# Layer 0's attention of images 0 to 6: from eight stretches of eight score tiles to five groups of thirteen

## The chip, the cores and the metric

The kernel runs on one core of one Trainium2 chip. The metric is the time of one execution on the device in microseconds (us). Three runs of the kernel before took 2767.86, 2767.95 and 2768.16 us, with a median of 2767.95. Engines are named as in the profile: PE is TensorE, PEld its weight loads, DVE is VectorE, ACT is ScalarE, POOL is GpSimd, SP is SyncE with its DMA queue.

## The reference

Eight images of 512 channels and 1024 tokens (32 by 32) in float32 pass through two attention blocks. What matters of block 0, with nh = 8 heads of ch = 64 channels:

```python
h = group_norm(x, gn_weight, gn_bias)
qkv = jnp.einsum('oc,bct->bot', w_qkv, h.reshape(B, C, T)) + b_qkv[None, :, None]
q, k, v = (qkv[:, :ch], qkv[:, ch:2 * ch], qkv[:, 2 * ch:])       # per head
weight = jnp.einsum('bct,bcs->bts', q * scale, k * scale)
weight = jax.nn.softmax(weight, axis=-1)
a = jnp.einsum('bts,bcs->bct', weight, v)
out = jnp.einsum('oc,bct->bot', w_proj, a) + b_proj[None, :, None]
return x + out
```

Block 1 is the same form with one head over all 512 channels and a group norm of 8 groups. The change touches block 0's attention and, because small products of block 1's group norm are computed in the middle of it, the place of those.

## The kernel before

The dense products (queries, keys, values, projections, and everything of block 1) are made with a Strassen-Winograd scheme, and the stages of neighbouring images are interleaved: while image b's block 0 attention runs, the block 1 norm of image b - 1 is worked in beside it. The program is written in one order. The recording layer keeps it on each engine (`keep_in_program_order` pins what could be moved), and each engine executes its own instructions in that order, waiting on semaphores for the others.

Block 0's attention of one image is `attention0` (L677). The eight heads are four pairs `hp`, the 1024 queries two halves `tb`, so there are eight stretches `(hp, tb)`, and each has eight tiles `s` of 128 keys. For one tile PE makes the scores of both heads side by side: the contraction has 64 rows, so the two heads sit in the two row halves of the array (shape 64*128 in the profile). The tile is 128 by 1024 and fills two banks of PSUM. ACT turns it into `e` with one exponential of 1024 columns (L696), DVE adds it to the running `total` of the stretch (L698 the first time, L700 after). After the eight score tiles of a stretch PE multiplies the eight `e` tiles with the values; here each head has 64 output channels, so the two heads sit in the two column halves of the array (shape 128*64), accumulating in `av`. ACT copies `av` to `a` (L719).

After every second stretch the totals of one head pair are ready. `reciprocals` (L631) sums each over the 128 partitions with a product with ones in quarters of the array (shape 128*32, tile `sums`), DVE copies the result to SBUF (`line`, L655), a DMA writes it to memory, another reads it back spread over the partitions (`cols`), DVE takes reciprocals (`recs`, L662), and two more DMAs bring them back as rows (`r`). DVE then multiplies `a` with `r` (L734), and SP stores `a` as `kept`. The last pair's scaling is moved behind the attention and done on POOL.

PSUM has eight banks. In this stage three pools of one two-bank tile hold the scores, taken in turn, and two banks (`acc_tile`) hold `av`, `sums`, and the group norm's `gmean` and `gvar`. So the scores of a tile can start when ACT has read the tile three before.

`big_tile` gives SBUF tiles of 4 KB per partition from one pool of `NBIG` = 34: images, queries, keys, values, `e` tiles, totals and factor sums all come from it.

Other work is hooked in through `extra`, sixteen lists of small steps taken in turn: an even slot between the scores and the values of a stretch, an odd slot behind its values. For images 1 to 6 the previous image's `projection2` fills them: POOL's residual additions (L1091) in slot 0, the norm's statistics on DVE in slots 1 and 3 and the store of the image to DRAM in 3, the group mean (`gmean`, L108 to 119) in slot 4, the affine factors (`gvar`, L121 to 130) in 5, and the norm's application on ACT in slots 7 and 9. The main loop adds to slots 9, 11, 13 and 15 the sums of the next products: DVE's `t_h` and `x` differences of 128 by 512 (L1028) and `inner_h` differences of 128 by 256 (L434).

Image 7, the last, goes through the same function without a store.

Of the kernel before, what the change touches and what calls it, by code (L numbers as in the profile page):

```python
# [9 lines left out]
F32 = mybir.dt.float32  # L10
I32 = mybir.dt.int32
AF = mybir.ActivationFunctionType
# [3 lines left out]
P = 128  # L16
EPS = 1e-5
ORDER = (1, 5, 2, 6, 7, 3, 4)
NBIG = 34

# [7 lines left out]
def two_attention_blocks_kernel(  # L30
# [28 lines left out]
    def matmul(*args, **kw):  # L59
        tc.keep_in_program_order(nc.tensor.matmul(*args, **kw))  # L60
# [113 lines left out]
    def main_path(ctx):  # L174
# [15 lines left out]
        def pair_tile(name):  # L190
            return big_tile(name, (P, 2, HT))

        def acc_tile(name):
            return ps_acc.tile([P, HT], F32, tag="acc", name=name)
# [433 lines left out]
            return out  # L628


        def reciprocals(totals, uid, across, direct=None):  # L631

            n = len(totals)
            sums = acc_tile(f"sums_{uid}")[:, : n * 2 * P].rearrange("p (t a b) -> p t a b", t=n, a=2)
            for t in range(n):  # L640
                for i in range(4):
                    matmul(
                        sums[ts(i, 32), t, :, :], ones, totals[t][:, :, ts(i, P)],
                        start=t == 0, stop=t == n - 1, skip_group_check=True,
                    )
            rows = all_rows[len(taken) : len(taken) + n]
            taken.extend(totals)
            line = rpool.tile([P, 2, 2, P], F32, tag="line", bufs=1, name=f"line_{uid}")[:, :n]
            queue = direct or nc.sync
            lines = lambda d: d.rearrange("t j i n -> i (t j) n"), line[0:P:32].rearrange("p t a b -> p (t a) b")  # L650
            if direct:
                nc.vector.reciprocal(line, sums)
                queue.dma_start(lines[0](rows), lines[1])
            else:
                nc.vector.tensor_copy(line, sums)  # L655
                raw_rows = rowpool.tile([n, 2, 4, P], F32, tag=f"rows{n}", name=f"rows_{uid}")
                queue.dma_start(lines[0](raw_rows), lines[1])
                cols = small.tile([P, 16], F32, tag="cols", name=f"cols_{uid}")[:, : n * 8]
                flat = lambda t: t.rearrange("t j i n -> (t j i n)").rearrange("(p m) -> p m", p=P)
                queue.dma_start(cols, flat(raw_rows))  # L660
                recs = small.tile([P, 16], F32, tag="recs", name=f"recs_{uid}")[:, : n * 8]
                nc.vector.reciprocal(recs, cols)  # L662
                queue.dma_start(flat(rows), recs)
            if across:
                r = pair_tile(f"r_{uid}")
                for j in range(2):
                    row = rows[0, j : j + 1].rearrange("j i n -> j (i n)")
                    queue.dma_start(r[:, j, :], row.to_broadcast([P, HT]))
            else:
                r = rpool.tile([P, 2, HT], F32, tag="r", bufs=1, name=f"r_{uid}")[:, :n]  # L670
                for j in range(2):
                    row = rows[:, j : j + 1].rearrange("t o i n -> o t (i n)")
                    queue.dma_start(r[ts(j, 64)], row.to_broadcast([64, n, HT]))
            return r


        def attention0(b, q, k, v, a, extra, store=None):  # L677
            n = 0
            scaled, totals, behind = [], [], []

            for hp in range(KC):
                for tb in (0, 1) if hp < KC - 1 or store else (1, 0):
                    uid = f"0_{b}_{hp}_{tb}"
                    total = pair_tile(f"sum_{uid}")
                    es = []
                    for s in range(NS):

                        sc = ps_pools[(0, 2, 1)[n % 3]].tile([P, 2, HT], F32, tag="sc", name=f"sc_{uid}_{s}")
                        n += 1
                        for j in range(2):  # L690
                            matmul(
                                sc[:, j, :], k[hp][ts(j, 64), ts(s, P)], q[hp][ts(j, 64), ts(tb, HT)],
                                start=True, stop=True,
                            )
                        e = pair_tile(f"e_{uid}_{s}")
                        nc.scalar.activation(e, sc, AF.Exp, scale=(C // 8) ** -0.5)  # L696
                        if s == 1:
                            nc.vector.tensor_add(total, es[0], e)  # L698
                        elif s > 1:
                            nc.vector.tensor_add(total, total, e)  # L700
                        es.append(e)
                    for f in extra.pop(0) if extra else ():
                        f()
                    av = acc_tile(f"av_{uid}")
                    for s in range(NS):
                        for j in range(2):
                            matmul(
                                av[ts(j, 64), :], v(s, 2 * hp + j),
                                es[s][:, j, :], start=(s == 0), stop=(s == NS - 1),
                            )  # L710
                    after = extra.pop(0) if extra else []
                    if not (store and hp == KC - 1):
                        after, scaled = [*scaled, *after], []
                    elif tb == 1:
                        after, scaled = [*after, *scaled], []
                    for f in after:
                        f()
                    dst = a[hp][:, ts(tb, HT)]
                    nc.scalar.copy(dst, av)  # L719

                    totals.append(total)
                    if hp < KC - 1 or store:
                        if tb == 0:
                            continue
                        dst = a[hp].rearrange("p (t n) -> p t n", t=2)
                    else:
                        dst = dst.rearrange("p (t n) -> p t n", t=1)
                    direct = store is None and (hp, tb) == (KC - 1, 0)
                    engine = nc.gpsimd if hp == KC - 1 and not direct else nc.vector
                    scaled = []  # L730

                    def scale(hp=hp, dst=dst, totals=totals, uid=uid, direct=direct, engine=engine, scaled=scaled):
                        r = reciprocals(totals, uid, False, nc.scalar if direct else None)
                        scaled.append(lambda: tc.keep_in_program_order(engine.tensor_tensor(dst, dst, r, ALU.mult)))  # L734
                        if store:
                            scaled.append(lambda: store(hp))

                    totals = []
                    if store and hp == KC - 1:
                        behind.append(scale)  # L740
                    else:
                        scale()

            assert not extra
            return scaled, behind


# [336 lines left out]
        def projection2(b, inner, hooks):  # L1084
# [8 lines left out]
            def store():  # L1093
# [3 lines left out]

            stats = [lambda c=c: norm.stats(c, xt[c]) for c in range(KC)]
            applies = [lambda c=c: norm.apply(nc.scalar, xt[c], xt[c], c) for c in range(KC)]
            _, _, (mean,), (affine,) = norm_hooks(norm, f"1_{b}")  # L1100
            return xt, {
                0: [lambda c=c: residual(c) for c in range(KC)], 1: stats[:2], 3: [*stats[2:], store], 4: [mean],
                5: [affine], 7: applies[:2], 9: applies[2:],
            }

        def norm_hooks(norm, uid):

# [64 lines left out]
            )  # L1172
            values1(b, zf, ef, state["r"], xt, f"1_{b}", ahead)

        x1, plan = None, {}
        for b in range(B):
            extra = [[] for _ in range(2 * 2 * KC)]
            for i, fs in later.items():
# [3 lines left out]
            if b > 0:  # L1182
                h, uid = x1, f"h1_{b - 1}"
            else:
                h, loads, applies = begun(load_x, norm0, 1, "h0")
                uid = "h0_1"
                for f in loads:
                    f()
                plan = {2 * c + 3: [f] for c, f in enumerate(applies)}
            for i, fs in plan.items():  # L1190
                extra[i] += fs
            a = channel_tiles(f"a0_{b}")
# [13 lines left out]
            psum_pools(f"attention_{b}", 1)  # L1206

            if last:
                scaled, _ = attention0(b, q, k, v, a, extra)
                for f in steps[4:7]:  # L1210
                    f()
                psum_pools(f"products_{b}", 2)
# [9 lines left out]
                break  # L1222

            kept = apool.tile([KC, P, T], F32, tag="kept", name=f"kept_{b}")
            scaled, behind = attention0(b, q, k, v, a, extra, lambda hp: nc.sync.dma_start(kept[hp], a[hp]))
            for f in ih[4:]:
                f()
            psum_pools(f"products_{b}", 2)
# [32 lines left out]
            q, k = keys_and_queries(  # L1261
                b + 1, inner, norm0, [lambda c=c: load_a(c) for c in range(KC)], [factors_of_a], q_hooks
            )
            x1, plan = projection2(b, inner_a, p_hooks)
        hf, steps = image_factors(h, f"h1_{B - 1}")
        inner, sums2 = inner_factors(hf, f"h1_{B - 1}")
        for f in steps + sums2:
# [204 lines left out]
```

## Time and profile before

The profile is one execution of 2768.3 us, 0.35 us over the median of the three runs. Its span, from the first to the last instruction, is 2765.8 us, so 2.5 us lie around it.

| engine | busy us | share of the span | instructions |
|---|---|---|---|
| PE | 2753.6 | 100% | 13436 |
| PEld | 1762.1 | 64% | 13436 |
| DVE | 2045.6 | 74% | 3214 |
| POOL | 1291.4 | 47% | 1384 |
| ACT | 998.4 | 36% | 1307 |

The granted TensorE clock is 0.999 of full speed over the span. Of PE's time, `sc` (block 0's scores) takes 456.8 us and `av` (its values) 453.4 us, each in 2048 instructions: a product in float32 is two passes of the array, each with its own weight load. Busy PE does not mean PE at its peak: matmuls overlap, and their ends are modelled. The time of a stage is read from the chain, which lists the pieces of work one behind the other, with the start of each.

### The profile page before, as it was taken

To read this page: it belongs to the slowest core of one execution; us is meant where nothing else is said; L and a number is where in the kernel's file an instruction comes from. 1 tells how busy PE (TensorE), PEld (TensorE's weight loads), DVE (VectorE), ACT (ScalarE), POOL (GpSimd) and SP (SyncE) were. 2 spreads that over 40 slices of the span, in tenths; PEclk is the share of its full clock that TensorE was granted. 3 is DMA by queue.
4 is the path that set the end of the run, shared out by engine and by line. 5 is a ranking of instruction groups with operands and counts; after the bars stand their busy time and mean duration, and the time that the engine had idled before them with its cause. 6 is when DMAs were issued, how large, how long until landed. Compare 5 with 4: busy or idle time off the path is not lost.

```text
span 2765.8 us, 36809 instructions
## 1 busy us (share of the span) xinstructions
PE 2753.6 (100%) x13436; PEld 1762.1 (64%) x13436; DVE 2045.6 (74%) x3214; ACT 998.4 (36%) x1307; POOL 1291.4 (47%) x1384
## 2 busy tenths in 40 slices
PE   9999999999999999999999999999999999999999
PEld 5437736776376853868538694486844968348585
DVE  6587777777777777777777867777678776787776
ACT  1253454214632146312453125531255313633130
POOL 2313605745067440774307752176621766146763
PEclk9999999999999999999999999999999999999999
DMA  7827412344113441144401443114521145112302
GB/s 265 253 91 252 181 32 70 138 159 166 40 63 138 170 162 32 63 161 167 150 24 63 177 182 119 32 55 184 196 98 49 58 153 216 59 54 97 142 24 74
DMA packets 126070, 332.60 MB, mean 120 GB/s; under 512 B 19831, under 2 KB 64695, under 8 KB 114362
## 3 DMA queue, kind: packets, MB, share of 16 engines
q1 hardware_dynamic: 125294, 329.75, 33.6%
q8 instruction: 108, 1.77, 0.3%
q14 instruction: 80, 0.66, 0.1%
q10 hardware_dynamic: 588, 0.42, 0.1%
HBM read 258.14 MB, written 71.99 MB: 119 GB/s over the span
## 4 chain that ended last, share of the span: by engine, by line
PE 99%; DVE 1%; DMA 0%; issue 0%; SPq 0%; DVEq 0%
PE sc L60 16%; PE av L60 16%; PE psb_av L60 6%; PE psb L60 5%; PE psa_av L60 4%; PE psc_av L60 4%; PE psc L60 4%; PE psa L60 3%; PE psb_v L60 3%; PE psb_k L60 3%; PE psb_p L60 3%; PE psb_q L60 3%; PE psb_g L60 3%; PE psb_z L60 3%; PE psc_z L60 2%; PE psa_k L60 2%
## 5 line engine op out<-in xcount | busy, mean ns | idle before, releaser
L700 DVE TENSOR_TENSOR sum<-sum,e 128x1024 f32<-128x1024 f32 x384 | 473.9, 1234 | 35.5 <-ACT e L696 0.9
L696 ACT ACTIVATE e<-sc 128x1024 f32<-128x1024 f32 x512 | 476.1, 1053 | 63.1 <-PE sc L60 62.6
L60 PE MATMUL sc<-q,k 64*128 64x512 f32 x2048 | 456.8, 596 | 0.0
L60 PE MATMUL av<-e,v 128*64 128x512 f32 x2048 | 453.4, 595 | 0.0
L60 PEld LDWEIGHTS sc<-q,k 64*128 64x128 f32 x2048 | 190.1, 185 | 245.9 <-ACT e L696 120.9
L60 PEld LDWEIGHTS av<-e,v 128*64 128x64 f32 x2048 | 141.4, 137 | 299.0 <-issue 288.2
L434 POOL TENSOR_TENSOR inner_h<-x 128x256 f32<-128x256 f32 x16 | 14.8, 924 | 415.9 <-DVE x L1028 415.9
L698 DVE TENSOR_TENSOR sum<-e,e 128x1024 f32<-128x1024 f32 x64 | 79.9, 1249 | 103.6 <-ACT e L696 103.6
L719 ACT COPY a<-av 128x512 f32<-128x512 f32 x64 | 37.5, 586 | 320.1 <-PE av L60 280.6
L126 POOL TENSOR_TENSOR rstd<-ve,mhalf 128x4 f32<-128x4 f32 x16 | 18.8, 1177 | 274.0 <-DVE ve L124 274.0
L60 PE MATMUL psb<-inner,inner_h 128*128 128x256 f32 x448 | 115.6, 380 | 0.0
L60 PE MATMUL psa_av<-e,z 128*128 128x512 f32 x256 | 112.5, 592 | 0.0
L482 ACT COPY psb_v<-psa_v 128x512 f32<-128x512 f32 (+1 forms) x28 | 14.5, 517 | 232.5 <-DVE x L845 176.6
L60 PEld LDWEIGHTS psb<-inner,inner_h 128*128 128x128 f32 x448 | 84.5, 190 | 13.6 <-POOL inner L449 2.1
L60 PE MATMUL psb_z<-w_z,inner_h 128*128 128x128 f32 x672 | 87.5, 276 | 0.0
L60 PE MATMUL psb_g<-inner_h,w_m 128*128 128x256 f32 x336 | 84.9, 381 | 0.0
L776 ACT ACTIVATE e<-e 128x1024 f32<-128x1024 f32 x64 | 65.1, 1052 | 46.7 <-DVE e L766 25.6
L60 PEld LDWEIGHTS psb_z<-w_z,inner_h 128*128 128x128 f32 x672 | 81.4, 192 | 0.5
L60 PEld LDWEIGHTS psa_av<-e,z 128*128 128x128 f32 x256 | 47.4, 190 | 53.6 <-issue 51.7
L771 POOL TENSOR_TENSOR e<-e,e 128x512 f32<-128x512 f32 x64 | 79.3, 1271 | 2.0 <-DVE e L766 1.8
L571 POOL TENSOR_TENSOR v<-v,v 128x256 f32<-128x256 f32 x28 | 20.1, 726 | 125.3 <-DVE u_v L566 121.3
L820 POOL TENSOR_TENSOR t<-e,t 128x1024 f32<-128x1024 f32 x32 | 78.4, 2482 | 0.0
(443 smaller groups left out, 6138.0 us busy)
## 6 DMA issues: line engine op xcount, KB each, us to landing
r<-all_rows SPq DMA_DIRECT2D x78, 256.0 KB
x<-in_x SPq DMA_DIRECT2D x36, 512.0 KB
h<-in_x SPq DMA_DIRECT2D x32, 512.0 KB
spill<-x SPq DMA_DIRECT2D x32, 512.0 KB
x<-spill SPq DMA_DIRECT2D x32, 512.0 KB
out<-x SPq DMA_DIRECT2D x63, 256.0 KB
kept<-a SPq DMA_DIRECT2D x28, 512.0 KB
again<-kept SPq DMA_DIRECT2D x28, 512.0 KB
```

The source lines that it names most:

```text
L60: tc.keep_in_program_order(nc.tensor.matmul(*args, **kw))
L126: nc.gpsimd.tensor_tensor(rstd, ve, mhalf, ALU.pow)
L434: pin(engine.tensor_tensor(dst, x, y, ALU.subtract))
L482: nc.scalar.copy(ps["b"], ps["a"])
L571: nc.gpsimd.tensor_tensor(d, x, y, ALU.add)
L696: nc.scalar.activation(e, sc, AF.Exp, scale=(C // 8) ** -0.5)
L698: nc.vector.tensor_add(total, es[0], e)
L700: nc.vector.tensor_add(total, total, e)
L719: nc.scalar.copy(dst, av)
L771: nc.gpsimd.tensor_tensor(blocks(dst, r, cc)[0], blocks(x, r, cc)[0], blocks(y, r, cc)[0], ALU.add)
L776: nc.scalar.activation(e[c, cc, r], e[c, cc, r], AF.Exp, scale=scale)
L820: on = lambda *a: lambda: tc.keep_in_program_order(nc.gpsimd.tensor_tensor(*a))
```

## The change

`attention0` is rewritten around a flat list of 64 tiles, (stretch, s) in the old order. For images 0 to 6 it is cut into groups of `GROUP` = 13: tiles 0 to 12, 13 to 25, 26 to 38, 39 to 51 and 52 to 63. A group first makes all its scores, then all its values, across the borders of the stretches. Image 7 keeps groups of 8. The slots are still taken in turn, one when a stretch's last score tile is made and one when its last value product is made; in groups of 13 the order of these events is scores of stretch 0, values of 0, scores of 1 and 2, values of 1 and 2, scores of 3, values of 3, scores of 4 and 5, values of 4 and 5, scores of 6 and 7, values of 6 and 7.

The products of `sums` (head pairs 0 to 2) and of the norm (`gmean` behind group 0, `gvar` behind group 1) move to the ends of groups, and write a tile of the score pools, taken in turn with the score tiles, instead of an `acc_tile`. The sums of head pairs 0, 1 and 2 stand behind groups 1, 2 and 3. For image 7 `gmean` and `gvar` stand behind its second and third stretch. The statistics all move to slot 0, the store to slot 1, the second half of the norm's application to slot 10 (9 for image 7). For image 0 the applications move from slots 3, 5, 7, 9 to 4, 5, 7, 10. `NBIG` rises by one to 35.

```diff
-NBIG = 34
+GROUP = 13
+NBIG = 35
...
-        def reciprocals(totals, uid, across, direct=None):
+        def reciprocals(totals, uid, across, direct=None, tile=None):
...
-            sums = acc_tile(f"sums_{uid}")[:, : n * 2 * P].rearrange("p (t a b) -> p t a b", t=n, a=2)
+            sums = acc_tile(f"sums_{uid}") if tile is None else tile[:, 0, :]
+            sums = sums[:, : n * 2 * P].rearrange("p (t a b) -> p t a b", t=n, a=2)
...
+            size = GROUP if store else NS
...
+            def place():
+                n = places[0] % 3
+                places[0] += 1
+                return ps_pools[(0, 2, 1)[n]].tile([P, 2, HT], F32, tag="sc", name=f"sc_0_{b}_{places[0]}")
...
+            def scores(i, s):
...
+                sc = place()
+                for j in range(2):
+                    matmul(
+                        sc[:, j, :], k[hp][ts(j, 64), ts(s, P)], q[hp][ts(j, 64), ts(tb, HT)],
+                        start=True, stop=True,
+                    )
+                e = es[i, s] = pair_tile(f"e_{uid}_{s}")
+                nc.scalar.activation(e, sc, AF.Exp, scale=(C // 8) ** -0.5)
+                if s == 1:
+                    nc.vector.tensor_add(total, es[i, 0], e)
+                elif s > 1:
+                    nc.vector.tensor_add(total, total, e)
+                if s == NS - 1:
+                    slot()
...
+            for start in range(0, len(tiles), size):
+                group = tiles[start : start + size]
+                for i, s in group:
+                    scores(i, s)
+                for i, s in group:
+                    values(i, s)
+                for f in edges.pop(0) if edges else ():
+                    f(place)
+                while waiting:
+                    waiting.pop(0)(due, place())
...
-            _, _, (mean,), (affine,) = norm_hooks(norm, f"1_{b}")
+            steps = [
+                [lambda place: norm.group_mean(place()[:, 0, :KC])], [lambda place: norm.affine(place()[:, 0, :KC])],
+            ]
             return xt, {
-                0: [lambda c=c: residual(c) for c in range(KC)], 1: stats[:2], 3: [*stats[2:], store], 4: [mean],
-                5: [affine], 7: applies[:2], 9: applies[2:],
-            }
+                0: [*(lambda c=c: residual(c) for c in range(KC)), *stats], 1: [store], 7: applies[:2], 9 if b + 2 == B else 10: applies[2:],
+            }, steps
...
-                plan = {2 * c + 3: [f] for c, f in enumerate(applies)}
+                plan = {i: [f] for i, f in zip((4, 5, 7, 10), applies)}
```

More of the change, by code (lines that the diff above doesn't have):

```diff
@@ L674, in reciprocals @@
             return r
[L677 to L744, printed above, removed]
@@ new lines, in attention0, with slot, values, done @@
+        def attention0(b, q, k, v, a, extra, store=None, edges=()):
+            places, scaled, behind, waiting, due = [0], [], [], [], []
+            edges = list(edges)
+            size = GROUP if store else NS
+            order = [
+                (hp, tb) for hp in range(KC) for tb in ((0, 1) if hp < KC - 1 or store else (1, 0))
+            ]
+            tiles = [(i, s) for i in range(len(order)) for s in range(NS)]
+            es, av, totals = {}, {}, {}
+            def place():
+                n = places[0] % 3
+                places[0] += 1
+                return ps_pools[(0, 2, 1)[n]].tile([P, 2, HT], F32, tag="sc", name=f"sc_0_{b}_{places[0]}")
+            def slot():
+                for f in extra.pop(0) if extra else ():
+                    f()
+            def scores(i, s):
+                hp, tb = order[i]
+                uid = f"0_{b}_{hp}_{tb}"
+                if s == 0:
+                    totals[i] = pair_tile(f"sum_{uid}")
+                total = totals[i]
+                sc = place()
[12 more added lines that the diff above has]
+                    slot()
+            def values(i, s):
+                hp, tb = order[i]
+                if s == 0:
+                    av[i] = acc_tile(f"av_0_{b}_{hp}_{tb}")
+                for j in range(2):
+                    matmul(
+                        av[i][ts(j, 64), :], v(s, 2 * hp + j), es[i, s][:, j, :], start=(s == 0), stop=(s == NS - 1),
+                    )
+                if s == NS - 1:
+                    done(i)
+            def done(i):
+                hp, tb = order[i]
+                uid = f"0_{b}_{hp}_{tb}"
+                last = hp == KC - 1
+                if not (store and last):
+                    while due:
+                        due.pop(0)()
+                slot()
+                if store and last and tb == 1:
+                    while due:
+                        due.pop(0)()
+                dst = a[hp][:, ts(tb, HT)]
+                nc.scalar.copy(dst, av[i])
+                if not last or store:
+                    if tb == 0:
+                        return
+                    dst = a[hp].rearrange("p (t n) -> p t n", t=2)
+                    which = [totals[i - 1], totals[i]]
+                else:
+                    dst = dst.rearrange("p (t n) -> p t n", t=1)
+                    which = [totals[i]]
+                direct = store is None and (hp, tb) == (KC - 1, 0)
+                engine = nc.gpsimd if last and not direct else nc.vector
+                def scale(into, tile=None):
+                    r = reciprocals(which, uid, False, nc.scalar if direct else None, tile)
+                    into.append(lambda: tc.keep_in_program_order(engine.tensor_tensor(dst, dst, r, ALU.mult)))
+                    if store:
+                        into.append(lambda: store(hp))
+                if store and last:
+                    behind.append(lambda: scale(scaled))
+                elif store:
+                    waiting.append(scale)
+                elif direct:
+                    scale(scaled)
+                else:
+                    scale(due)
+            for start in range(0, len(tiles), size):
[8 more added lines that the diff above has]
+                    waiting.pop(0)(due, place())
+            assert not extra and not due
@@ L1099, in projection2 @@
             applies = [lambda c=c: norm.apply(nc.scalar, xt[c], xt[c], c) for c in range(KC)]
-            _, _, (mean,), (affine,) = norm_hooks(norm, f"1_{b}")
+            steps = [
+                [lambda place: norm.group_mean(place()[:, 0, :KC])], [lambda place: norm.affine(place()[:, 0, :KC])],
+            ]
             return xt, {
-                0: [lambda c=c: residual(c) for c in range(KC)], 1: stats[:2], 3: [*stats[2:], store], 4: [mean],
-                5: [affine], 7: applies[:2], 9: applies[2:],
-            }
+                0: [*(lambda c=c: residual(c) for c in range(KC)), *stats], 1: [store], 7: applies[:2], 9 if b + 2 == B else 10: applies[2:],
+            }, steps
         def norm_hooks(norm, uid):
@@ L1173, in layer1_rest @@
             values1(b, zf, ef, state["r"], xt, f"1_{b}", ahead)
-        x1, plan = None, {}
+        x1, plan, edges = None, {}, []
         for b in range(B):
@@ L1208, in main_path @@
             if last:
-                scaled, _ = attention0(b, q, k, v, a, extra)
+                scaled, _ = attention0(b, q, k, v, a, extra, None, [[], *edges])
                 for f in steps[4:7]:
@@ L1224, in main_path @@
             kept = apool.tile([KC, P, T], F32, tag="kept", name=f"kept_{b}")
-            scaled, behind = attention0(b, q, k, v, a, extra, lambda hp: nc.sync.dma_start(kept[hp], a[hp]))
+            scaled, behind = attention0(b, q, k, v, a, extra, lambda hp: nc.sync.dma_start(kept[hp], a[hp]), edges)
             for f in ih[4:]:
@@ L1263, in main_path @@
             )
-            x1, plan = projection2(b, inner_a, p_hooks)
+            x1, plan, edges = projection2(b, inner_a, p_hooks)
         hf, steps = image_factors(h, f"h1_{B - 1}")
```

## The prediction

> **What bounds the kernel now.** I read the page first (busy times and the chain that ended last), then that chain in order of time over one image's attention, then the weight loads of one stretch, then DVE around one border. The page gives PE 99% of the chain. DVE's running sums are long, but nothing idles long before them.
>
> ```profile
> PE 99%; DVE 1%; DMA 0%; issue 0%; SPq 0%; DVEq 0%
> L700 DVE TENSOR_TENSOR sum<-sum,e 128x1024 f32<-128x1024 f32 x384 | 473.9, 1234 | 35.5 <-ACT e L696 0.9
> ```
>
> The chain shows what a stretch costs. The first row below is a product of block 1 on the whole array: 16 passes of 512 columns in 6.87 us, 0.429 each. A score or value tile is four passes on half an array, two at a time, so 2 x 0.429 = 0.859 and eight tiles are 6.87 too.
>
> ```profile
> 1199.47 6.87 PE psa_av L60 x16
> ...
> 997.39 7.07 PE sc L60 x32
> 1004.46 7.02 PE av L60 x32
> 1011.48 7.07 PE sc L60 x32
> 1018.54 7.02 PE av L60 x32
> 1025.56 1.00 PE sums L60 x16
> 1026.56 7.07 PE sc L60 x32
> 1033.63 0.21 PE gmean L60 x4
> 1033.85 6.92 PE av L60 x32
> 1040.76 0.07 PE gvar L60 x3
> 1040.83 7.07 PE sc L60 x32
> ```
>
> So each entry into scores costs 0.20 us and each entry into values 0.15, the price of changing the array's shape: 0.35 a stretch. `gmean` between scores and values costs 0.21 - 0.10 = 0.11 (the values behind it are 0.10 shorter); `gvar` behind values, in the same shape, 0.07.
>
> The weight loads of one stretch, which starts at 1085.02 in this view, show how near ACT is to being the bound:
>
> ```profile
> L60 PE MATMUL sc<-q,k x2048: 589/589/693, 117.8 to 2456.7; 64*128 64x512 f32 x187
> ```
>
> ```profile
> 1088.18 0.19 PEld L60 LDWEIGHTS sc<-q,k 64*128 64x128 f32 x2 [0.29 <-ACT e L696]
> ...
> 1089.10 0.51 PEld L60 LDWEIGHTS sc<-q,k 64*128 64x128 f32 x4 [0.35 <-ACT e L696]
> 1090.01 0.45 PEld L60 LDWEIGHTS sc<-q,k 64*128 64x128 f32 x4 [0.41 <-ACT e L696]
> 1090.93 0.39 PEld L60 LDWEIGHTS sc<-q,k 64*128 64x128 f32 x4 [0.47 <-ACT e L696]
> ```
>
> These are the loads of tiles 4 to 7, each released by the exponential that frees its place. They are (1090.93 - 1088.18) / 3 = 0.917 us apart: ACT's pace, against PE's 0.859. Tile 7's first matmul is due at 1085.02 + 0.10 + 7 x 0.859 = 1091.13, so its load is only 0.20 ahead, and each further tile loses 0.058. A load needs 0.10: the first matmuls of a stretch, whose load nothing covers, last 693 ns and not 589. The stretch of eight ends just before ACT's pace is felt.
>
> DVE around the border behind the third head pair:
>
> ```profile
> 1068.11 1.22 DVE L734 TENSOR_TENSOR a<-a,r 128x1024 f32<-128x1024 f32 x1
> 1069.25 1.29 DVE L1028 TENSOR_TENSOR t_h<-x 128x512 f32<-128x512 f32 x2
> 1070.45 0.42 DVE L434 TENSOR_TENSOR inner_h<-x 128x256 f32<-128x256 f32 x1
> ...
> 1073.08 1.23 DVE L698 TENSOR_TENSOR sum<-e,e 128x1024 f32<-128x1024 f32 x1 [1.08 <-ACT e L696]
> 1074.41 7.87 DVE L700 TENSOR_TENSOR sum<-sum,e 128x1024 f32<-128x1024 f32 x6
> 1082.20 1.29 DVE L1028 TENSOR_TENSOR t_h<-x,t_h 128x512 f32<-128x512 f32 x2
> ...
> 1086.34 0.69 DVE L655 COPY line<-sums 128x512 f32<-128x512 f32 x1
> 1088.16 1.23 DVE L698 TENSOR_TENSOR sum<-e,e 128x1024 f32<-128x1024 f32 x1 [1.14 <-ACT e L696]
> 1090.42 0.25 DVE L662 RECIPROCAL recs<-cols 128x16 f32<-128x16 f32 x1 [1.03 <-DMA cols<-rows]
> ```
>
> `line` is already 1.3 us late here (sums end at 1085.0), which costs nothing while `sums` has a bank of its own. `recs` waits for its DMA, 4.08 us from the start of `line`, and holds DVE.
>
> **The change part by part.** Per image, times from a group's first score.
>
> *Fewer changes of shape.* Five pairs instead of eight. A pair without sums takes 14.09 (997.39 to 1011.48), 0.35 over 13.74; three go: -1.06. `gmean` stands in its own shape now, 0.07 instead of 0.21 - 0.10: -0.04 at least, -0.11 if it hides as `gvar` nearly does; I take -0.08 for images 1 to 6. The three sums stay at 1.0 each.
>
> *ACT's pace in long groups.* Tile 12's load comes 5 x 0.058 - (0.20 - 0.10) = 0.19 too late; PE waits that much in each of groups 0 to 3: +0.77. Group 4 has 12 tiles, 0.13, mostly swallowed by the stall below, during which ACT catches up: +0.03. Bounds per long group: 0.09 if a load needed no lead, 0.28 if it needs its recorded 187 ns. I take 0.10, which the trace shows for this shape. The Trainium skill, "TensorE: Matmul & The Clock Gate", section "LDWEIGHTS (loading the stationary operand)", puts a load at columns / 1.2 GHz, here 107 ns; an estimate from that page gives 0.20 a group against 0.28 by the recorded duration.
>
> A rule against the change is in the Trainium skill, "TensorEngine Tiling (Array Packing)", section "PSUM Bottleneck": packing speeds up PE but not the emptying of PSUM, which may become the bound. Read strictly, all 13 tiles would go at ACT's 0.917, 0.75 us over PE a group, 3.7 an image; but then a stretch of eight would already be 0.46 longer, and 7.07 is explained by the entry alone. The three places absorb the first eight tiles.
>
> *The small products in score places.* The third score tile of a group takes the place of the last small product, so it waits until DVE has read it, in DVE's order. The third tile's load is due 1.72 after the group's start. Behind group 0, DVE is at `gmean` after four sums of stretch 1: the seventh of stretch 0 starts 18.2 after the image's start (the statistics in front of it stand as before), five steps of 1.33 less the shorter join make 24.6; the group ends at 26 x 0.859 + 0.35 + 0.19 + 0.07 = 22.9, due 24.7. It just fits: +0.05, bounds 0 and 0.4. Behind groups 1 and 2 DVE has two to four us in hand.
>
> *The border behind group 3 is the tight one.* DVE's queue there, in the changed program's order: `line` of pair 1 at 0.1; one sum at 2.2; `recs`, held by its DMA until 0.1 + 4.1 = 4.2; seven sums from 4.4, 9.12 long (1073.08 to 1082.20): 13.5; `t_h` 1.20: 14.7; `inner_h` x4 1.47: 16.2; three sums 3.8: 20.0; `a` times `r` 1.14: 21.1; `t_h` 1.21: 22.3; eight `inner_h` 2.93 (1083.41 to 1086.34): 25.3; then `line`, read out at 25.95. The group with its sums takes 22.33 + 0.35 + 0.19 + 1.0 = 23.87, so the load is due at 25.6: PE waits 0.4. Bounds: 0 (DVE 0.4 faster) and 1.3 (`recs` 5.0 behind `line`, as behind image 0's first and last pair). I take 0.4, by the 4.0 to 4.3 of the waits on `cols` before a last pair. Behind this wait on PE stand ten score tiles and group 4's values; DVE's own sums wait with them.
>
> *At nothing.* ACT's norm applications (slots 7, 10; 4, 5, 7, 10 in image 0) and `av` copies stand behind a group's exponentials, under 11 us of values; before an exponential each application would cost about 1.05. SP's order is unchanged; the stores of `a` wait longer for DVE, and the one `e` tile that reuses a stored `a` needs it 10 us into group 4, some 8 us after it can land. `e` tiles reuse tiles whose sums are over in the group before. DVE ends group 4 no later than the sums of pair 3 need, as 11 sums fit into 21 us.
>
> **Sum.** Images 1 to 6: -1.06 - 0.08 + 0.80 + 0.05 + 0.4 = +0.11 each, +0.7. Image 0, without the norm: +0.14. Image 7: up to +0.1 for the norm's tiles. Together +0.9 on the profiled 2768.3, or 2768.9 against the median of 2767.95 (0.35 lower than the profiled run).
>
> **Rivals.** (A) *Waits vanish*: the lead is shorter and DVE in time. Per image -1.14 + 0.38 + 0.05 = -0.7, seven images -5: 2763; with no cost at all -8: 2760. For it: the smallest bounds; against it: 693 ns. (B) *DVE's queue at the fourth border* is later by 1 us (a slower DMA, or steps as long as beside POOL's work: two `t_h` took 2.35 at 1112.63 and 1.29 above): +1 x 7 on the sum, 2776. It crosses the 0.2% from 0.7 us of extra lateness on. For it: every item in that queue adds directly, and the last pair's `recs` come 4.8 after `line`; against it: POOL is nearly idle there. (C) *ACT's pace from the first tile*: 64 x 0.058 = 3.7 an image instead of 0.8: +20, 2788. Against it: 7.07. (D) *Waits of the longer-living tiles* (DMA, SBUF tiles) that I count as covered: like B in size.
>
> **How the numbers follow.** 0.2% is 5.5 us, about what a measurement of this kernel tells from no change. Likeliest, gains and waits nearly cancel: 0.72, 2768.9, own range 2764 to 2773. A beyond 5.5 us: 0.07. B and D: 0.18. C: 0.03. The range 2763 to 2777 leaves out part of A, and of B and D what is over 2777, and C. Faster 0.07, same 0.72, slower 0.21.
>
> **What would show it.** In the changed profile: pieces of 13 score tiles of 11.55 us (11.17 + 0.20 + 0.19) and of 13 value tiles of 11.3; in images 0 to 6 a wait of PE for DVE's `line` L657, seven times, about 0.4; nothing new outside the attention. The prediction is wrong if score pieces are near 11.9 (ACT binds earlier), or if that wait is over 1 us or absent.

## The result, and the profile after

The changed kernel takes 2776.37 us (median of eight runs, 2773.68 to 2778.99); beside it the kernel before took 2767.94. The ratio is 1.003, 95% interval 1.0019 to 1.0041: slower, by 8.4 us or 0.3%, where the prediction called 0.2% a difference (the interval's lower end, 0.19%, just touches that). Its runs lie 5.3 us apart, where those of the kernel before lay 0.7 us apart. The profiled execution took 2774.31 us with a span of 2772.5, 6.0 and 6.7 us more than the profiled one of before.

The chain of work that ended last, summed by engine, from the page of the changed kernel:

```profile
PE 94%; DVE 3%; DMA 1%; ACT 1%; issue 1%; DVEq 0%; SPq 0%; ACTq 0%
```

PE was 99% of the chain and is 94% now: in a few places something other than PE's own work ended last. It is not the attention of a later image. Here is the chain in order of time over that of image 3 (start us, us, what):

```profile
1001.67 11.61 PE sc L61 x52
1013.28 11.31 PE av L61 x52
1024.59 11.69 PE sc L61 x55
1036.27 11.31 PE av L61 x52
1047.58 12.62 PE sc L61 x71
1060.20 11.31 PE av L61 x52
1071.51 12.56 PE sc L61 x68
1084.08 11.31 PE av L61 x52
1095.38 11.78 PE sc L61 x64
1107.16 10.45 PE av L61 x48
1117.61 1.06 PE psa_g L61 x4
```

Thirteen tiles at 0.859 are 11.17 us. Value pieces last 0.14 more, the entry. Score pieces last 0.44 more, the entry of 0.20 and 0.24 of ACT's pace. The pieces of 71, 68 and 64 instructions contain 16 of `sums`, those of 55 and 71 three of the norm. All in all 1117.61 - 1001.67 = 115.94 us, against 1113.26 - 997.39 = 115.87 before: +0.07.

Reading the same two starts in every image gives, for images 0 to 7, +0.41, +0.59, +0.21, +0.07, +0.09, +0.08, +0.19 and +0.10, together 1.74 us. The remaining 5 us of the span are in three places: 3.0 us in the v product that follows image 0's attention, 0.3 in image 7's block 1, and 1.6 at the very end, after DVE's last operation. What lies around the span became 0.7 us shorter, which leaves 6.0.

The largest of the three shows in PE's waits over the whole span (engine, line, what was waited for: us in total, times, longest), the first row of the kernel before, the others of the changed one:

```profile
PE psb_v L60 <- DVE u_v L566: 0.5, 1, 0.5
```

```profile
PE psb_v L61 <- DVE u_v L567: 3.6, 2, 3.2
PE sc L61 <- DVE line L657: 0.7, 2, 0.5
PE psb L61 <- ACT u L473: 0.3, 1, 0.3
```

Why `u_v` is late is read from DVE's timeline behind image 0's attention (start us, us, the operation; in brackets the idle time before it and what ended that), first before, then after the change:

```profile
236.86 0.68 DVE L655 COPY line<-sums 128x512 f32<-128x512 f32 x1
...
241.89 0.24 DVE L662 RECIPROCAL recs<-cols 128x16 f32<-128x16 f32 x1
243.12 0.76 DVE L566 TENSOR_TENSOR u_v<-psb_v,v 128x256 f32<-128x256 f32 x2 [0.99 <-PE psb_v L60]
```

```profile
237.35 0.68 DVE L657 COPY line<-sums 128x512 f32<-128x512 f32 x1
...
247.55 0.25 DVE L664 RECIPROCAL recs<-cols 128x16 f32<-128x16 f32 x1 [5.12 <-DMA cols<-rows]
247.72 0.69 DVE L567 TENSOR_TENSOR u_v<-psb_v,v 128x256 f32<-128x256 f32 x2
```

The reciprocals stand in DVE's queue ahead of `u_v` in both. Before, their `cols` had landed when DVE came to them, 5.0 us behind `line`. Now DVE waits 5.12 us for `cols`, which land 10.2 us behind `line`. What the queue of SP does there says why (DMA issues: start us, time of the issue, what, how many), before and after:

```profile
215.21 8.84 SPq L314 DMA_DIRECT2D sums_z<-prepare_z  x7
224.21 1.65 SPq L348 DMA_DIRECT2D w_v<-sums_v  x1
229.15 0.33 SPq L348 DMA_DIRECT2D w_k<-sums_k  x1
...
237.57 0.57 SPq L657 DMA_DIRECT2D rows<-line  x1
239.75 0.31 SPq L660 DMA_DIRECT2D cols<-rows  x1
```

```profile
221.92 9.06 SPq L315 DMA_DIRECT2D sums_z<-prepare_z  x7
231.14 1.36 SPq L349 DMA_DIRECT2D w_v<-sums_v  x1
236.00 0.33 SPq L349 DMA_DIRECT2D w_k<-sums_k  x1
...
238.06 0.56 SPq L659 DMA_DIRECT2D rows<-line  x1
245.83 0.31 SPq L662 DMA_DIRECT2D cols<-rows  x1
```

The order is the same in both. A burst of 6.1 MB (seven stores of 448 KB, loads of 1344 and 1792 KB) stands on SP behind the small DMAs of head pair 2. The change puts pair 2's sums behind group 3, which ends four tiles after that pair's last tile, so the burst starts 6.7 us later. The last pair's sums come where they came before (238.06 against 237.57). The distance between `w_k` and `rows` shrinks from 8.4 us to 2.1, and the 8 KB write that took 2.2 us, from the issue of `rows` to that of `cols`, which waits for its landing, takes 7.8. The times at which landings raise semaphores, which the trace also has, say the same: before, `w_k` had landed by 236.7, ahead of `rows`; now it lands from 243.9 to 244.9, and the last of `rows` at 245.8.

### The profile page after: what moved, and what is told of

Its sections match the earlier page's. It is cut to its first block, busy times and chain, and to the rows that moved or that the text cites. A ratio compares the mean times of both kernels' runs of the same rounds, so it can differ in the third digit from the quotient of the medians.

```text
span 2772.5 us, 36801 instructions
## 1 busy us (share of the span) xinstructions
PE 2754.6 (99%) x13436; PEld 1756.1 (63%) x13436; DVE 2039.6 (74%) x3214; ACT 995.5 (36%) x1307; POOL 1290.5 (47%) x1384
## 4 chain that ended last, share of the span: by engine, by line
PE 94%; DVE 3%; DMA 1%; ACT 1%; issue 1%; DVEq 0%; SPq 0%; ACTq 0%
PE sc L61 15%; PE av L61 14%; PE psb_av L61 6%; PE psb L61 5%; PE psc_av L61 4%; PE psa_av L61 4%; PE psc L61 3%; PE psa L61 3%; PE psb_k L61 3%; PE psb_q L61 3%; PE psb_p L61 3%; PE psb_g L61 3%; PE psb_z L61 3%; PE psb_v L61 3%; PE psc_z L61 2%; PE psc_k L61 2%
## 5 line engine op out<-in xcount | busy, mean ns | idle before, releaser
L61 PEld LDWEIGHTS sc<-q,k 64*128 64x128 f32 x2048 | 179.7, 185 | 260.0 <-ACT e L711 172.8
L61 PE MATMUL psb_v<-w_v,inner_h 128*128 128x128 f32 x588 | 76.2, 276 | 3.6 <-DVE u_v L567 3.6
```

## The experiments

The theory after the trace, T: the shifted burst behind image 0 makes most of the loss and of the spread between runs. The rival, B, as in the prediction: each image with groups of 13 loses about 1.2 us at its borders, in waits too small to be listed. Each kernel below was timed beside the kernel before, and differences are from the median of that there (2768.21, 2768.31 or 2768.06).

### Image 0 in eights, or image 0 alone in thirteens

```diff
-            size = GROUP if store else NS
+            size = GROUP if store and b > 0 else NS
```

> The changed kernel, but image 0 goes in groups of 8 tiles and images 1 to 6 stay in groups of 13. Theory T (collision behind image 0): the sums of head pair 2 stand one group of 5 tiles later in image 0, SP issues the burst behind them (seven stores of 448 KB and two weight loads) some 6.7 us later, the small round trip of the last pair's sums runs into it (4.1 us become 10.2), and DVE, held by its reciprocals, comes 3 us late with what image 1's v product waits for; on other executions more. With image 0 in eights the burst is back where it was: 2769 to 2771, PE's wait for u_v back at about 0.5, and executions within 1.5 us of each other. Theory B (the rival of the prediction: each image with groups of 13 loses about 1.2 at its borders): six of seven images are left, 2775.

```diff
-            size = GROUP if store else NS
+            size = GROUP if store and b == 0 else NS
...
-                0: [*(lambda c=c: residual(c) for c in range(KC)), *stats], 1: [store], 7: applies[:2], 9 if b + 2 == B else 10: applies[2:],
+                0: [*(lambda c=c: residual(c) for c in range(KC)), *stats], 1: [store], 7: applies[:2], 9: applies[2:],
...
-            scaled, behind = attention0(b, q, k, v, a, extra, lambda hp: nc.sync.dma_start(kept[hp], a[hp]), edges)
+            scaled, behind = attention0(b, q, k, v, a, extra, lambda hp: nc.sync.dma_start(kept[hp], a[hp]), [[], *edges])
```

> The mirror: image 0 alone in groups of 13, images 1 to 6 in groups of 8 (norm's tiles in slots of eights, all else of the change kept). Theory T: the loss is in this image, so 2772 to 2778, executions several us apart, and DVE's reciprocals at the end of image 0's attention wait 4 us or more for their DMA. Theory B: one image of seven, 2769.

Measured: 2772.03 us (2770.94 to 2773.11, 11 runs; ratio 1.0014, interval 1.0005 to 1.0023) and 2776.29 us (2773.77 to 2779.09, 6 runs; 1.0031, 1.0018 to 1.0043). With the small products left in score places, image 0 alone in thirteens brings back nearly the whole loss (+8.1) and the whole spread; how much of that is the place, the next run shows. PE's waits, image 0 in eights first:

```profile
PE psb_v L61 <- DVE u_v L567: 0.5, 1, 0.5
```

```profile
PE psb_v L61 <- DVE u_v L567: 3.9, 2, 3.5
```

B falls: six of seven images in thirteens cost +3.8, less than half of the loss. But +3.8 and not the +1 to +3 that T allowed, so something else costs too.

### No group of thirteen

```diff
-            size = GROUP if store else NS
+            size = NS
```

(with the two lines on `applies` and `edges` as in the diff above, so that the norm keeps its distance in groups of eight)

> No group of 13 at all: the size is 8 in every image, but the other half of the change is kept (the sums' and gmean's products in score places, one more tile of the SBUF pool). It prices that half. Theory T: no late burst, executions within 1.5 us; PE may wait for DVE's line at each pair's border, as the sums now stand in a score place, up to 0.5 an image: 2768 to 2771. Theory B: 2768, as the groups are gone.

Measured: 2771.51 us (2770.46 to 2772.48, 11 runs; 1.0012, 1.0003 to 1.0021), +3.3 without any group of 13. The other half of the change, the small products in score places, has a price of its own. In image 3 the attention is 0.29 us longer than before; from the weight loads' waits there, and from the chain:

```profile
PEld sc L61 <- DVE line L657: 0.9, 1, 0.9
```

```profile
1087.42 0.61 DVE line L657
...
1088.08 5.42 PE sc L61 x24
```

At pair 2's border `line` is read out of the score place at 1088.03, behind DVE's `inner_h` differences, and the third score tile waits for that place. The images read 0.29, 0.29, 0.29, 0.29, 0.54 and 0.64 (1 to 6), so 0.3 to two thirds of a microsecond each.

### The sums in a bank of their own

```diff
-            size = GROUP if store else NS
+            size = NS
...
-                while waiting:
-                    waiting.pop(0)(due, place())
+                while waiting:
+                    waiting.pop(0)(due)
```

(and the two lines on `applies` and `edges` as above)

> Groups of 8 in every image and the sums in a bank of their own again; of the change only gmean's and gvar's place, the norm's slots, the order of sums and norm at a border and the 35th tile are left. Eights with the sums in score places measured +3.3 us, 0.3 to 0.6 an image, with PE waiting for DVE's line at a border. If that place is the cause, 2767.5 to 2769 here, and no wait of PE for line; if the 3.3 us come from the norm's place or the slots, 2771 again.

Measured: 2768.61 us (2768.09 to 2770.69, 11 runs; 1.0002, 0.9993 to 1.0011), +0.3 and not to be told from the time of before. PE has no wait for `line` in the list, and images 1 to 4 and 6 are each about 0.05 us shorter than before (image 5 is 0.20 longer). So 3.0 of the 3.3 us belong to the place of the sums. What the norm's products, its slots and the 35th tile cost is at most small: the span is 1.0 us longer than before (2766.8 against 2765.8), with a wait of PE for DVE's `x` of 0.5 that the kernel before does not have, while less lies around the span.

### The burst ahead of pair 2's small DMAs

```diff
-                3: steps, 4: [load], 5: second[:1], 7: second[1:2], 9: second[2:3], 11: second[3:4], 12: [
+                3: steps, 4: [load], 5: second[:1], 7: second[1:2], 8: second[2:3], 9: second[3:4], 11: [
```

> The changed kernel, all groups of 13, but in image 0 the four sum tiles, and with the last of them the burst of stores and weight loads, are made one or two slots earlier, so that SP issues the burst ahead of pair 2's small DMAs. Theory T: the burst is over before the last pair's round trip, PE's wait for u_v falls from 3.6 to below 1, 2769 to 2772, and executions within 2 us of each other. Theory B: nothing changes at the groups' borders, 2775 to 2777.

Measured: 2777.88 us (2777.18 to 2778.43, 5 runs; 1.0035, 1.0021 to 1.0049), slower than the changed kernel. The wait for `u_v` did go, to 0.8, and the spread shrank to 1.3 us; but the collision moved to the pair before. SP's queue, DVE's wait and PE's:

```profile
219.49 2.50 SPq L349 DMA_DIRECT2D w_v<-sums_v  x1
224.46 0.33 SPq L349 DMA_DIRECT2D w_k<-sums_k  x1
224.83 0.57 SPq L659 DMA_DIRECT2D rows<-line  x1
232.26 0.31 SPq L662 DMA_DIRECT2D cols<-rows  x1
```

```profile
DVE recs L664 <- DMA cols<-rows: 12.6, 2, 10.1
```

```profile
PE sums L61 <- DVE sum L715: 3.5, 1, 3.5
```

Pair 2's `line` was ready at 214.6, but its `rows` stand behind `w_k`, which SP cannot issue until 224.46 (the place of `w_k` in SBUF is freed when the stores of `sums_z` have landed; the chain has "217.63 6.78 DMA sums_z<-prepare_z" just ahead). Issued 0.4 us behind `w_k`, they take 7.4. DVE stands 10.1 us, so the running sums are late, and with them PE. The expectation overlooked that pair 2's round trip is as exposed as the last pair's. The mechanism is the same, the edit no remedy.

The stall has a second price here. PE stands from 235.65 to 239.17, and soon after that the granted clock falls to half for 3.41 us (the stretch, then the busy times of PE, PEld, DVE, ACT and POOL, the clock, the DMA share and GB/s):

```profile
240.45:243.86 3.41, 3.41 (x19) 3.41 (x18) 3.41 (x5) 1.17 (x2) 2.42 (x3) 0.50 0.02 7
```

By estimate that is 1.7 us of PE's work lost. The profiled executions of the changed kernel and of image 0 alone in thirteens, with stalls of 3.2 and 3.5 us, show no such stretch, so what decides on it is not known from these runs.

### One load of the burst behind the last pair's round trip

```diff
                 queue.dma_start(cols, flat(raw_rows))
+                if uid == f"0_0_{KC - 1}_1":
+                    load_k()
...
-                    second[4], load, load,
+                    second[4], load,
...
-                ],
+                ], "k": load,
...
+        load_k = later.pop("k")
```

> The changed kernel, all groups of 13, with one load of the burst behind image 0 moved: w_k (1792 KB, a third of the 6.2 MB) is issued behind the last pair's cols instead of ahead of its rows. The run before showed that moving the whole burst ahead of pair 2 only moves the collision to that pair's round trip. Theory T: what is left (4.4 MB from 221.9, some 13 us at 330 GB/s) has landed when the last pair's rows go out at 238, so rows and cols take near 4 us instead of 9.4, PE's wait for u_v falls from 3.6 to below 1, 2771 to 2774, executions within 3 us of each other. If size is not what matters (the round trip is slow for another reason, or image 0's 4.6 us lie elsewhere): 2775 to 2778 as the change has it.

Measured: 2770.94 us (2770.56 to 2771.46, 11 runs; 1.0009, 1.0000 to 1.0018), +2.6 where the changed kernel stands at +8.4: 5.8 us less, with all groups of 13 in place, and 0.9 us between the runs in place of 5.3. SP and DVE:

```profile
231.05 1.42 SPq L349 DMA_DIRECT2D w_v<-sums_v  x1
...
238.14 0.56 SPq L659 DMA_DIRECT2D rows<-line  x1
240.83 0.31 SPq L662 DMA_DIRECT2D cols<-rows  x1
241.26 0.37 SPq L349 DMA_DIRECT2D w_k<-sums_k  x1
```

```profile
237.43 0.68 DVE L657 COPY line<-sums 128x512 f32<-128x512 f32 x1
...
242.63 0.25 DVE L666 RECIPROCAL recs<-cols 128x16 f32<-128x16 f32 x1 [0.58 <-DMA cols<-rows]
```

With `rows` issued at the same time as in the changed kernel, `recs` follow `line` by 5.2 us and not 10.2, and PE's wait for `u_v` is 0.5 as before the change. The profiled execution of the changed kernel showed 3.0 us of this; its other runs lie up to 4.7 us above that one. Since moving one load takes the spread away too, I put the whole difference down to the collision: 3 to 8 us from run to run, 5.8 in the median. Part of that may be the clock: of the eight runs the three with a mean granted clock of 0.998 took 2776.20, 2777.77 and 2778.99, those with 0.999 took 2773.68 to 2777.11. Only the profiled run has a trace, so this is not shown.

### The round trip on another queue

```diff
-                queue.dma_start(lines[0](raw_rows), lines[1])
+                trip = nc.scalar if uid == f"0_0_{KC - 1}_1" else queue
+                trip.dma_start(lines[0](raw_rows), lines[1])
...
-                queue.dma_start(cols, flat(raw_rows))
+                trip.dma_start(cols, flat(raw_rows))
```

> The changed kernel with the burst where it is; only the two small DMAs of image 0's last pair (rows<-line and cols<-rows, 8 KB each) are issued on ACT's queue instead of SP's. Two accounts of the slow round trip. Queue: the 8 KB stand behind w_k's 1792 KB, issued 2 us before them on the same queue; on a queue of their own they pass it, line to recs falls from 10.2 us to about 5, PE's wait for u_v below 1, 2770.5 to 2772.5. Bandwidth: all 16 DMA engines are busy (share 0.95 to 1.04) and any transfer waits, whichever queue issues it; then recs wait 4 to 5 us as in the changed kernel, 2775 to 2778. The Trainium skill, "DMA: Bandwidth & Descriptors", section "Queues, rings and completion order", says that SP's and ACT's queues have rings of their own, which each DMA engine serves in turn a packet at a time (the first account); its section "Issuing engines are not separate DMA queues" says that another issuing engine saves only the time to issue (nearer the second).

Measured: 2776.08 us (2775.20 to 2776.85, 8 runs; 1.0028, 1.0017 to 1.0039). ACT's queue issues:

```profile
238.08 1.13 ACTq L660 DMA_DIRECT2D rows<-line  x1
...
245.70 0.35 ACTq L663 DMA_DIRECT2D cols<-rows  x1
```

From `rows` to `cols` 7.62 us, where SP's queue had 7.77: nothing is gained by a queue of its own. `cols` waits there on more than one semaphore, and the profile puts the end of ACT's wait down to one that `w_k` raises. But the trace also has the times at which landings raise the semaphore of `rows`: the last ones at 244.5 to 245.6, just before `cols` goes out at 245.70, and among those of `w_k` (243.9 to 246.2, so `cols` did not wait for all of that). So the 8 KB themselves landed with the large load and not ahead of it. The account by queues, as the expectation put it, falls; of the two sections of the Trainium skill's "DMA: Bandwidth & Descriptors" named there, "Issuing engines are not separate DMA queues" is the one that these 7.62 us agree with. Why taking turns packet by packet did not let the 8 KB pass, no run here shows.

The run is not a clean swap of queues. SP, no longer held by `cols`, issues two loads of 512 KB (`ahead`) at 237.95 and 238.43; they landed after `rows` (246.5 to 250.0), but `cols` comes behind them, and `recs` follow `line` by 12.8 us and not 10.2. The granted clock is 0.50 here too, from 247.06 to 250.47. New besides: ACT, held by the wait, comes late with its copies for the v product (PE waits 2.9 and 1.4 us for them).

## Why the prediction was half right

By medians the loss comes apart so: the sums' place +3.0 (+3.3 with the rest of that half), groups of 13 in images 1 to 6 a further +0.5 (their intervals overlap, so this is not clear of noise), image 0 in groups of 13 a further +4.6. The range of 2763 to 2777 held the time by luck: its upper part was kept for B and D, B did not come, D had no place, and the time lies 0.6 us below its end. The likeliest time, 2768.9 with a range of its own up to 2773, was wrong, and "slower", with a chance of 0.21, is what came.

**What held.** The attention itself, predicted at +0.9 in sum, showed +1.74 in the profile. Pieces of 13 score tiles were to last 11.55 us and last 11.61; of values 11.3 and 11.31. ACT's pace was put at 0.19 a group, between 0.09 and 0.28: 11.61 - 11.37 = 0.24, and 12.56 - 1.0 - 11.37 = 0.19. The strict reading of the rule on emptying PSUM, 0.75 a group, is refuted for these groups by the same 0.19 to 0.24, and of the two figures for a group, 0.20 by the Trainium skill's page ("TensorE: Matmul & The Clock Gate", section "LDWEIGHTS (loading the stationary operand)") and 0.28 by the recorded duration, the first is the nearer. The place of `gmean` (+0.05): 11.69 - 11.61 = 0.08 with the 0.07 of its own passes in it. Rival C (+20) and, in the attention, B are out.

**What was mis-sized.** The wait for `line` behind group 3, 0.4 in each of seven images. The list has 0.7 us in two waits, 0.2 in image 0 and 0.5 in image 1, and image 3's group 4 lasts 11.78 where 10.31 + 0.20 + 1.0 = 11.51 are its work; so 0.27 with ACT's pace in it. The wait exists, at about half the price. Why the place costs more in groups of eight was not looked for.

**What failed.** Under "at nothing" the prediction says "SP's order is unchanged". It is, and that is the fault: the order was checked and the times were not. The burst keeps its place behind pair 2's small DMAs, so it moves 6.7 us with them, while the last pair's stay. The other half of the same step is the duration used for a round trip, 4.0 to 4.3 us, with 5.0 as the bound "as behind image 0's first and last pair". In the kernel before, nothing over 512 KB was issued in the 8 us ahead of any `rows`; here it was, and the trip took 10.2. Rival D, waits on DMA that are counted as covered, comes nearest, but it was about longer-living tiles, had no place and borrowed its price from B.

**What nothing in the prediction covers.** After DVE's last operation the kernel runs on for 6.3 us instead of 4.7. The same 6.0 to 6.3 stand in the four other kernels with images 1 to 6 in thirteens, and 4.8 to 4.9 in the three without. With `w_k` moved this is +1.3 in the span, against which 0.8 less lies around the span; +2.6 in all. In the changed kernel it stands in the closing instructions: DVE's last DRAIN starts 1.73 us after ACT's (2772.19 against 2770.46), where before the two start 0.02 us apart. The cause is open. It also hides that, with the sums in score places, the groups do gain in images 1 to 6: their attention sums to 1.2 us over that of before in thirteens with image 0 in eights, and to 2.3 in eights, which is 0.2 us an image.

No version here beats the kernel before: with `w_k` moved the change stands at +2.6 us, and what brings it back to before is taking the groups and the sums' place out.

## What to carry to other kernels

An unchanged order on a queue does not say that a move is free: when a step shifts, list what stands behind it on that queue, shift it by as much, and look whether a small round trip that something waits for now falls into it. One such meeting, behind one image of eight, cost more than all seven regrouped attentions. A small product that moves into a shared place takes on the reader's lateness: its price is how far the reader is behind when the place is next wanted, and a trace with a bank to spare shows that lateness as free.

## What the runs showed of the hardware

An 8 KB write (from the issue of `rows` to that of `cols`) took 1.7 to 1.8 us behind the other head pairs of the kernel before, with nothing over 100 KB issued in the 9 us ahead of it. Behind the last pairs of images 0 to 6 it took 2.2, with a 512 KB store issued 0.55 us ahead; the 1792 KB load issued 8.4 us ahead of image 0's added nothing to that. It took 2.7 with a load of 1344 KB 7.1 us ahead besides, and 7.4 to 7.8 with a load of 1792 KB 0.4 to 2.1 us ahead, and landed among the last of that load or just after it. It landed no sooner from ACT's queue (7.5, from 238.1 to 245.6). The DMA engines' busy share hardly tells the two apart: from 235 to 240 us it is 1.04 with 421 GB/s in the changed kernel, where the write took 7.8 us, and 0.93 with 373 GB/s with `w_k` moved, where it took 2.7. What differs is what was issued just ahead.

In two of the kernels a stall of PE (3.5 us, and 1.4 and 2.9 us close together) was followed by 3.41 us at a granted clock of 0.50; in two others a stall of 3.2 and of 3.5 us was not.
